# Diagonal blocks of the scores copied by ScalarE, and small sums moved behind a read of PSUM, in a two-layer graph kernel

## The chip, the cores and the metric

The kernel runs on one core of a Trainium2 chip. Time is device time in microseconds (us) of one execution; the profile is of one further execution and uses the hardware profiler's records. The engines are named as in the profile: PE is TensorE's matrix products, PEld its weight loads, DVE is VectorE, ACT is ScalarE, POOL is GpSimd, SP is SyncE, which here only issues transfers (DMAs). A trailing q (SPq, DVEq) means the engine's instruction queue and not its arithmetic.

## The reference

There are 64 graphs of 256 nodes with 512 features, one adjacency matrix of zeros and ones for all, and two residual layers with a layer norm and a ReLU ahead of each:

```python
h = jnp.maximum(_layernorm(x, axis=-1), 0.0)
q, k, v = h @ Wq.T, h @ Wk.T, h @ Wv.T
rel = adj.T[None] * einsum('bnd,bmd->bnm', q, k)
rel = rel / norm(rel, axis=2)
x = x + einsum('bnm,bmd->bnd', rel, v)          # layer 0
h = jnp.maximum(_layernorm(x, axis=-1), 0.0)
x = x + (einsum('nm,bmd->bnd', adj, h) @ weight + bias)   # layer 1
```

## The kernel before

The 64 graphs are worked through as 32 pairs. For a pair i the steps are: h, the norm of x; ht, its transpose; g, the product of h with the matrix m (which holds Wq and Wk multiplied beforehand); v, the product with Wv; the scores rel, from h and g; attention, which adds rel times v to x; h2, the second norm; y, the gather of h2 over the adjacency matrix; and the mix, which multiplies y with the weight and adds to x. Pairs overlap: `steady(i)` (L1009), called for i = 1 to 28, does attention and the second layer of pair i, the scores of pair i + 1, g and v of pair i + 2 and the transposes of pair i + 3. `first_pairs` and `last_pairs` (L1057) fill and drain this.

The large products are done by Winograd's scheme of seven products of half size with sums of blocks ahead of and behind them (`winograd_steps`, L187), and for g, v and mix two of the seven are split again (`two_levels`, L212). The seven are called a1, c5, a6, a7, a4 (large ones, into the PSUM banks bank_a and bank_c) and g1 to g4 (groups of small ones, into bank_d and bank_e). Each step issues its matmuls and then the instruction that reads the bank: ScalarE copies the first result for a block (`take`, L467 for g, L516 for v), VectorE adds a later one (L776 for mix). As bank_a is used again and again, a product into it waits until the bank has been read.

The order of every engine's instructions is written by hand and is kept as written (`manual_schedule`, L904). `run_steps` (L280) runs a list of steps, and behind step n it runs what the dictionary `side` has under n; "slot n" means that place. What waits for what is found by the framework from the pieces of tiles that instructions read and write, and becomes waits on semaphores.

The scores of a pair end in `rel`, 128 partitions (the row n within half k of the nodes) with all 256 columns m. Attention needs them transposed. VectorE's transpose (L592, `turn`) turns each 32x32 block on its own, so the blocks have to be moved first: block (j, k) of every 128x128 square goes from partitions 32k.. and columns 32j.. of `rel` to partitions 32j.. and columns 32k.. of `placed`. `place` (L584) does it with 16 transfers from SP's queue, one for each (j, k), each of 32 partitions x 8 runs of 32 numbers. In the 4 of them with j = k the partitions and columns don't change. Ahead of `place`, ScalarE has squared the scores into `placed` as a scratch (L570), taken the root, and scaled `rel` (L582). Behind it VectorE's four `turn`s write `turned`.

In `steady`, `place` is in slot 0 of `g_and_v` (L918), right behind the scaling; the turns are in slot 3 of the gather (`run_steps(y_products, ...)`, L1042), behind the last of y's four products. Just ahead of the turns on VectorE stands the first sum of y, L176 (slot 2); just behind it the second, L177, whose result mix's product c5 uses. `g_and_v` has seven steps: slot 5 lies behind v's c5 (ScalarE: v<-bank_c, L516) and slot 6 behind g's a4 and g3 (ScalarE: g<-bank_a, L467); next on ScalarE come the four copies of y out of PSUM (L746). SP's queue in an iteration holds 16 transfers of `place_blocks` (L443, from `h`), one load of x, and then the 16 of `place`; next it waits for the h of the next iteration.

In the tail, `second_of_y` (L758) gives eight small sums of y (128x128, L176 to L179), which the small products of mix take: the first four of the list hold the sums for g1, the last four those for g2 and g3. For the last two pairs (b and c in `last_pairs`) they are put into slots of the mix: four behind a1 and four behind c5 for pair b, all eight behind c5 for pair c.

Of the kernel before, what the change touches and what calls it, by code (L numbers as in the profile page):

```python
# [19 lines left out]
def kernel(  # L20
# [38 lines left out]
    nc = tc.nc  # L59
    P = 128  # L60
# [10 lines left out]
    S = 32  # L71
# [7 lines left out]
    small = ctx.enter_context(tc.tile_pool(name="small", bufs=3))  # L79
    ps_m = ctx.enter_context(tc.tile_pool(name="ps_m", bufs=8, space=bass.MemoryType.PSUM))  # L80

    X, H, HL, G, V, R, H2, Y, HL2, Y2, second_h = ({} for _ in range(11))

    ring = [const.tile([P, NB, NC, D], F32, name=f"x_ring{n}") for n in range(5)]
    blocks = const.tile([P, TC, DC, P], F32, name="blocks")
# [34 lines left out]
    def flat(t):  # L120
        return t.rearrange("p b c d -> p (b c) d")
# [154 lines left out]
    def winograd(product, take, side={}, early=False):  # L276

        run_steps(winograd_steps(product, take, early), side)
# [30 lines left out]
    def product_of_tokens(left, right):  # L309

        def product(bank, n, start):
            for b in range(NB):
                for d in range(HC):
                    nc.tensor.matmul(  # L314
                        bank[:, ts(b, P)], right[n][:, d, ts(b, P)], left[n][:, d, ts(b, P)],
                        start=(start and b == 0 and d == 0), stop=(d == HC - 1),
                        skip_group_check=True,
                    )
        return product
# [180 lines left out]
    def g_operands(i, room=None):  # L500

        g = G[i]
        if room is None:
            t = work.tile([P, 3, HC, HT_], F32, tag="ys", name=f"gt_{i}")
            room = [t[:, n] for n in range(3)]
        G[i], steps = right_operands(lambda j, k: g[:, j * HC : (j + 1) * HC, k], room)
        return steps
# [34 lines left out]
        products = v_products(i)  # L542
        return two_levels(*products, *second_weights_moving(HL2[i], wv_second, V[i]))

    def scores(i, side={}, by_matmul=False, inside=False):

        left, right = HL.pop(i), G.pop(i)
        rel = work.tile([P, NB, NC, N], F32, tag="rel", name=f"rel_{i}")  # L550
        placed = work.tile([P, NB, NC, NC, P], F32, tag="placed", name=f"placed_{i}")
        turned = work.tile([P, NB, NC, NC, P], F32, tag="turned", name=f"turned_{i}")
        rn = small.tile([P, NB, NC], F32, tag="rn", name="rn")
        R[i] = turned, rel, placed

        def take(t, k, bank, first):
            dst = rel[:, :, k, ts(t, P)]
            src = bank[:, :HT_].rearrange("p (b m) -> p b m", b=NB)
            if first:
                nc.scalar.copy(dst, src)  # L560
            else:
                nc.vector.tensor_add(dst, src, dst)  # L562

        def mask(k):
            nc.vector.tensor_mul(
                rel[:, :, k], rel[:, :, k], adjt_sb[:, k : k + 1, :].to_broadcast([P, NB, N])
            )

        def square_sum(b, k):
            nc.scalar.activation(  # L570
                placed[:, b, k].rearrange("p t n -> p (t n)"), rel[:, b, k], AF.Square,
                accum_out=rn[:, b, k : k + 1],
            )

        def root():
            nc.scalar.activation(rn, rn, AF.Sqrt)

        def inverse():
            nc.vector.reciprocal(rn, rn)

        def scale(b, k):
            nc.scalar.activation(rel[:, b, k], rel[:, b, k], AF.Copy, scale=rn[:, b, k : k + 1])  # L582

        def place():  # L584
            rv = rel.rearrange("p b k (t m) -> p (b k t) m", m=P)
            pv = placed.rearrange("p b k t n -> p (b k t) n")
            for j in range(P // S):
                for k in range(P // S):
                    nc.sync.dma_start(out=pv[ts(j, S), :, ts(k, S)], in_=rv[ts(k, S), :, ts(j, S)])  # L589

        def turn(b, k):
            nc.vector.transpose(turned[:, b, :, k], placed[:, b, k])  # L592

        def each(f):
            return [(lambda b=b, k=k: f(b, k)) for k in range(NC) for b in range(NB)]

        def turn_at_once():
            for b in range(NB):
                pt = ps_m.tile([P, T], F32, tag="pm", name="pr")
                for t in range(NC):  # L600
                    for k in range(NC):
                        nc.tensor.transpose(
                            pt[:, ts(t * NC + k, P)], rel[:, b, k, ts(t, P)], ident
                        )
                nc.scalar.copy(turned[:, b].rearrange("p t k n -> p (t k n)"), pt)

        masks, squares = [lambda: mask(0), lambda: mask(1)], each(square_sum)
        if inside:
            side = by_slot(side, {5: masks[1:], 6: squares[2:]})
            masks, squares = masks[:1], squares[:2]  # L610
        winograd(product_of_tokens(left, right), take, side)
        if by_matmul:
            return masks, squares, root, inverse, rn, turn_at_once
        return (
            masks, squares, root, inverse, each(scale), place,
            each(turn),
        )
# [185 lines left out]
    def by_slot(*works):  # L803

        side = {}
        for work_items in works:
            for n, items in work_items.items():
                side[n] = side.get(n, []) + list(items)
        return side
# [199 lines left out]
    def steady(i, exact, relu0, v_last, mixed, v):  # L1009

        gs = g_operands(i + 1)
        relus0 = relus_of_h(i + 3, relu0)
        stats, root, end, relus, uppers, lowers = ln1(i, exact)
        halves = [stats[b * NC + t] for t in range(NC) for b in range(NB)]
        attend_and_v(i, mixed, v, {
            0: relus0[0:2] + v_last, 1: relus0[2:4] + gs[0:1], 2: gs[1:2],
            3: gs[2:3], 4: gs[3:4] + halves[0:1], 5: halves[1:2],  # L1020
        })
        place_blocks(i + 3)
        if i + 4 < NP:
            load(i + 4)
        HL2.pop(i + 1)
        h_second = second_h.pop(i + 2)()
        masks, squares, norm_root, inverse, scales, place, turns = scores(i + 1, {
            0: halves[2:3], 1: halves[3:4] + h_second[0:1], 2: [root] + h_second[1:4],
            3: [end] + relus[0:1], 4: relus[1:2],
        }, inside=True)  # L1030
        turned, sums = transpose_blocks(i + 3)
        v_steps, rel_steps = attend_operands(i + 1)
        g, v = g_and_v(i + 2, {
            0: masks + squares + [norm_root] + turned[0:4] + [inverse] + scales + [place],
            1: uppers[0:2] + lowers[0:2],
            2: relus[2:4],
            3: uppers[2:4] + turned[4:8],
            4: lowers[2:3] + sums[0:1] + add_bias(i),
            5: lowers[3:4] + sums[1:3], 6: sums[3:4] + v_steps[0:1],
        })  # L1040
        y_products, y_steps = gather_steps(i, exact)
        run_steps(y_products, {0: v_steps[1:2], 2: y_steps[0:1], 3: turns})  # L1042
        y_second = second_of_y(i)
        totals, row_squares, mean, root0, end0, relu0 = [], [], [], [], [], None
        if i + 4 < NP:
            totals, *middle, relu0 = norm_by_scalar(flat(X[i + 4]))
            mean, row_squares, root0, end0 = [middle[0]], middle[1], [middle[2]], [middle[3]]
        run(y_steps[1:2])
        mixed = mix_and_v(i, g, v, {
            0: y_steps[2:4] + totals[0:2], 1: y_second[0:4] + totals[2:4],  # L1050
            2: y_second[4:8] + mean + row_squares[0:2],
            3: rel_steps[0:2] + row_squares[2:4], 4: root0 + rel_steps[2:4] + end0,
            5: v_steps[2:3],
        })
        return relu0, v_steps[3:4], mixed, v

    def last_pairs(exact, relu0, v_last, mixed, v):  # L1057

        a, b, c = NP - 3, NP - 2, NP - 1
        gs = g_operands(b)  # L1060
        stats, root, end, relus, uppers, lowers = ln1(a, exact)
# [18 lines left out]
        y_steps = gather(a, exact)  # L1080
# [6 lines left out]
        y_second = second_of_y(a, "hs2")  # L1087
# [7 lines left out]
        m = mix_by_two_levels(a)  # L1095
        root, end, relus, uppers, lowers = parts
# [9 lines left out]
        y_products, y_steps = gather_steps(b, exact)  # L1106
        run_steps(y_products, {2: y_steps[0:1]})
        y_second = second_of_y(b, "hs2")
# [5 lines left out]
        m = mix_by_two_levels(b)  # L1114
        root, end, relus, uppers, lowers = parts
# [1 line left out]
            m["a1"], m["c5"], m["a6"], m["g1"], lambda: run([m["a7"], m["c"]]), m["g2"], m["a4"],  # L1117
            m["g3"],
        ], {
            0: y_second[0:4] + [root], 1: y_second[4:8] + [end] + relus[0:2] + uppers[0:2],  # L1120
            4: lowers[0:2] + relus[2:4], 5: uppers[2:4] + add_bias(c), 7: lowers[2:4],
        })
        y_products, y_steps = gather_steps(c, exact)
        run_steps(y_products, {0: [m["g4"]], 2: y_steps[0:1]})
        y_second = second_of_y(c, "hs2")
        run(y_steps[1:2])
        m = mix_by_two_levels(c)
        run_steps([
            m["a1"], m["c5"], m["a6"], m["g1"], lambda: run([m["a7"], m["c"]]), m["g2"], m["a4"],
            m["g3"], m["g4"],  # L1130
        ], {0: y_steps[2:4], 1: y_second})

    first = dict(X), H[0]
    with tc.If(inexact < 1) as either:
# [33 lines left out]
```

## Time and profile before

| what | us |
|---|---|
| timed runs: median of 3 (lowest to highest) | 1706.56 (1706.11 to 1707.01) |
| the profiled execution: its own time | 1703.48 |
| its span, from first to last instruction | 1701.4 |
| PE busy in it | 1684.2 |
| DVE busy | 1472.9 |
| ACT busy | 811.3 |
| issue of one transfer placed<-rel on SP, least / median / most | 0.585 / 0.609 / 1.804 |
| from its issue to its landing, least / median / most | 1.9 / 2.0 / 4.0 |

A line in order of time has: start in us from the span's start, length in us, engine, source line, operation, output<-inputs by the program's names, shape, number of instructions put together, and in brackets the idle time of the engine ahead of it with what ended it. A line of the chain of waits has only start, length and what. In the busy table, x is the number of instructions. Matmuls are pipelined: the next one can start before the last has ended, so starts tell more than lengths. The granted TensorE clock was 0.999 of full speed.

### The profile page before, as it was taken

The numbers are of one execution on the slowest core, as the hardware profiler recorded it, in microseconds if no ns is written. First come the engines' busy times: TensorE is split into PE (matmuls) and PEld (weight loads), VectorE is DVE, ScalarE is ACT, GpSimd is POOL, SyncE is SP. The second block draws the span as 40 slices with busy tenths as digits, with TensorE's granted clock in tenths as the row PEclk, the third lists the DMA queues.
The fourth block names the chain that finished last, engine by engine and source line by source line (L and its number), as shares of the span: only waits on it lengthen the run. The fifth ranks groups of instructions, "written<-read, shape, count | busy, mean of one in ns | idle before, by whom it ended". The sixth has DMA issues, their size and how long they took to land.

```text
span 1701.4 us, 28459 instructions
## 1 busy us (share of the span) xinstructions
PE 1684.2 (99%) x10274; PEld 1530.6 (90%) x10274; DVE 1472.9 (87%) x3312; ACT 811.3 (48%) x1835; POOL 226.7 (13%) x191
## 2 busy tenths in 40 slices
PE   9999999999999999999999999999999999999997
PEld 7979999999899999999999999999999999999986
DVE  7788889888898888898888988888988889888677
ACT  4455444545445554445544455454455544453331
POOL 1211100111101111001111001110011110011111
PEclk9999999999999999999999999999999999999999
DMA  7414332234332233332343322443323433223101
GB/s 247 63 26 87 84 78 57 55 77 87 79 62 68 53 87 85 77 60 63 65 87 80 83 50 50 87 87 77 60 67 60 87 83 80 55 47 62 38 25 53
DMA packets 425734, 122.56 MB, mean 72 GB/s; under 512 B 398064, under 2 KB 398832, under 8 KB 425584
## 3 DMA queue, kind: packets, MB, share of 16 engines
q1 hardware_dynamic: 412992, 80.28, 25.6%
q0 software_dynamic: 8432, 32.51, 5.2%
q10 hardware_dynamic: 4160, 7.87, 1.3%
q8 instruction: 83, 1.36, 0.3%
q14 instruction: 67, 0.55, 0.1%
HBM read 38.27 MB, written 33.55 MB: 42 GB/s over the span
## 4 chain that ended last, share of the span: by engine, by line
PE 91%; DVE 4%; SPq 2%; DMA 1%; ACT 1%; issue 1%; DVEq 0%; ACTq 0%
PE bank_a L302 24%; PE bank_a L290 12%; PE bank_a L314 7%; PE bank_c L302 6%; PE bank_e L528 6%; PE bank_a L665 6%; PE py L742 6%; PE bank_d L528 5%; PE bank_c L314 3%; PE bank_c L290 3%; PE bank_c L665 3%; PE bank_e L481 3%; SPq L589 2%; PE bank_d L481 2%; PE bank_b L314 2%; PE bank_b L665 1%
## 5 line engine op out<-in xcount | busy, mean ns | idle before, releaser
L726 POOL TENSOR_TENSOR x_ring<-x_ring,bias_bc 128x512 f32<-128x512 f32 x128 | 187.2, 1483 | 667.3 <-DVE rel L562 406.2
L302 PE MATMUL bank_a<-wv_t,ht 128*128 128x256 f32 x768 | 181.7, 379 | 0.0
L290 PE MATMUL bank_a<-ht,m_t 128*128 128x256 f32 x768 | 181.4, 379 | 0.0
L290 PEld LDWEIGHTS bank_a<-ht,m_t 128*128 128x128 f32 x768 | 145.9, 190 | 19.8
L302 PEld LDWEIGHTS bank_a<-wv_t,ht 128*128 128x128 f32 x768 | 143.5, 190 | 18.3
L714 DVE TENSOR_TENSOR h<-h2c,h 128x512 fp32r<-128x512 f32 x128 | 85.4, 689 | 80.0 <-ACT h L710 80.0
L516 ACT COPY v<-bank_a 128x512 f32<-128x512 f32 x96 | 55.1, 574 | 206.5 <-PE bank_a L302 206.5
L367 ACT ACTIVATE blocks<-x_ring,sm 128x512 f32<-128x512 f32 x112 | 80.8, 722 | 125.3 <-DVE sm L364 123.5
L742 PE MATMUL py<-adjt_r,h 128*128 128x256 f32 x1024 | 127.1, 281 | 0.5 <-DVE h L714 0.4
L345 ACT ACTIVATE h2c<-x_ring,nb,rs 128x512 f32<-128x512 f32 x128 | 97.3, 809 | 58.0 <-DVE nb L342 51.9
L302 PE MATMUL bank_a<-w_t,ys 128*128 128x256 f32 x512 | 121.4, 380 | 2.2 <-DVE x_ring L776 2.2
L742 PEld LDWEIGHTS py<-adjt_r,h 128*128 128x128 f32 x1024 | 120.9, 189 | 1.0 <-DVE h L714 0.9
L797 POOL DMA_DIRECT2D out_dram<-x_ring x31 | 24.0, 773 | 723.3 <-issue 522.9
L380 ACT ACTIVATE h<-x_ring,nb,rs 128x512 f32<-128x512 f32 x112 | 82.0, 802 | 66.0 <-PE bank_e L528 66.0
L302 PEld LDWEIGHTS bank_a<-w_t,ys 128*128 128x128 f32 x512 | 96.7, 190 | 16.4 <-DVE x_ring L776 3.0
L746 ACT COPY yt<-py 128x512 f32<-128x512 f32 x128 | 74.9, 588 | 70.4 <-PE py L742 47.3
L776 DVE TENSOR_TENSOR x_ring<-bank_a,x_ring 128x512 f32<-128x512 f32 x128 | 87.9, 687 | 23.2 <-PE bank_a L302 23.2
L314 PE MATMUL bank_a<-ht,gt 128*128 128x128 f32 x744 | 101.2, 279 | 0.0
L333 DVE BATCH_NORM_STATS2 st<-x_ring 128x6 f32<-128x512 f32 x144 | 97.6, 678 | 0.4
L560 ACT COPY rel<-bank_a 128x256 f32<-128x256 f32 x96 | 35.7, 372 | 129.6 <-PE bank_a L314 111.1
L314 PEld LDWEIGHTS bank_a<-ht,gt 128*128 128x128 f32 x744 | 90.4, 192 | 2.8
L453 DVE STREAM_TRANSPOSE ht<-blocks 128x256 f32<-128x256 f32 x248 | 87.7, 407 | 0.7 <-DMA blocks<-h 0.7
(223 smaller groups left out, 4012.5 us busy)
## 6 DMA issues: line engine op xcount, KB each, us to landing
blocks<-h SPq DMA_DIRECT2D x496, 64.0 KB, 2.3
out_dram<-x_ring POOLq DMA_DIRECT2D x31, 1024.0 KB, 4.8
x_ring<-in_x_dram SPq DMA_DIRECT2D x28, 1024.0 KB, 5.6
placed<-rel SPq DMA_DIRECT2D x496, 32.0 KB, 2.0
x_ring<-in_x_dram ACTq DMA_DIRECT2D x4, 1024.0 KB, 5.3
wq_sb<-in_L_gnn_Wq_dram SPq DMA_DIRECT2D x4, 256.0 KB, 4.8
wk_sb<-in_L_gnn_Wk_dram ACTq DMA_DIRECT2D x4, 256.0 KB, 6.0
wv_sb<-in_L_gnn_Wv_dram ACTq DMA_DIRECT2D x1, 1024.0 KB, 5.6
```

Of the source, the lines that this page charges most:

```text
L290: nc.tensor.matmul(bank[:, e * HT_ : (e + 1) * HT_], right[n][:, d, ts(e, P)], left[n][:, d, :], start=(start and e == 0 and d == 0), stop ...
L302: nc.tensor.matmul(bank[:, b * HD : (b + 1) * HD], left[n][:, d, ts(b, P)], right[n][:, d, :], start=(start and b == 0 and d == 0), stop=( ...
L314: nc.tensor.matmul(bank[:, ts(b, P)], right[n][:, d, ts(b, P)], left[n][:, d, ts(b, P)], start=(start and b == 0 and d == 0), stop=(d == H ...
L333: nc.vector.bn_stats(st[:, c, :], src[:, c, :])
L345: nc.scalar.activation(dst, src[:, c, :], AF.Relu, bias=nb[:, c : c + 1], scale=rs[:, c : c + 1])
L453: nc.vector.transpose(ht[:, d, half].rearrange("p (b n) -> p b n", b=NB), by_half[:, :, half, d])
L528: nc.tensor.matmul(out, left[k][n], right[k][n], start=start, stop=True, skip_group_check=True)
L665: nc.tensor.matmul(bank[:, ts(b, HD)], left[n][:, b], right[n][:, b], start=(start and b == 0), stop=True, skip_group_check=True,)
L714: nc.vector.tensor_sub(dst[:, 1, c, :], whole_h[c], dst[:, 0, c, :].bitcast(F32))
L726: (lambda c=c: add(xt[:, c, :], xt[:, c, :], bias_bc, ALU.add)) for c in range(TC)
L742: nc.tensor.matmul(pm[:, d, :], left[:, b * NC + m, ts(d0 + d, P)], right, start=(n == 0), stop=(n == len(terms) - 1),)
L776: nc.vector.tensor_add(xt[block], bank.rearrange("p (b e) -> p b e", b=NB), xt[block])
```

## The change

Two edits. In `steady`, the scores are called with `own=True`: `place` then leaves out the four transfers with j = k, and four ScalarE copies of the same blocks (`stay`) are put into slots 5 and 6 of `g_and_v`, two in each, ahead of the other side work there. `first_pairs` and `last_pairs` keep the 16 transfers. In `last_pairs`, the eight small sums of y move back by one slot: for pair b from slots 0 and 1 to slots 1 and 2, for pair c the last four from slot 1 to slot 2. What is computed doesn't change.

```diff
-    def scores(i, side={}, by_matmul=False, inside=False):
+    def scores(i, side={}, by_matmul=False, inside=False, own=False):
...
+        rv = rel.rearrange("p b k (t m) -> p (b k t) m", m=P)
+        pv = placed.rearrange("p b k t n -> p (b k t) n")
+
         def place():
-            rv = rel.rearrange("p b k (t m) -> p (b k t) m", m=P)
-            pv = placed.rearrange("p b k t n -> p (b k t) n")
             for j in range(P // S):
                 for k in range(P // S):
-                    nc.sync.dma_start(out=pv[ts(j, S), :, ts(k, S)], in_=rv[ts(k, S), :, ts(j, S)])
+                    if j != k or not own:
+                        nc.sync.dma_start(
+                            out=pv[ts(j, S), :, ts(k, S)], in_=rv[ts(k, S), :, ts(j, S)]
+                        )
+
+        def stay(j):
+            nc.scalar.copy(pv[ts(j, S), :, ts(j, S)], rv[ts(j, S), :, ts(j, S)])
+
+        own_steps[i] = [(lambda j=j: stay(j)) for j in range(P // S)]
...
-        }, inside=True)
+        }, inside=True, own=True)
...
-            5: lowers[3:4] + sums[1:3], 6: sums[3:4] + v_steps[0:1],
+            5: own_steps[i + 1][0:2] + lowers[3:4] + sums[1:3],
+            6: own_steps[i + 1][2:4] + sums[3:4] + v_steps[0:1],
...
-            0: y_second[0:4] + [root], 1: y_second[4:8] + [end] + relus[0:2] + uppers[0:2],
+            0: [root], 1: y_second[0:4] + [end] + relus[0:2] + uppers[0:2], 2: y_second[4:8],
...
-        ], {0: y_steps[2:4], 1: y_second})
+        ], {0: y_steps[2:4], 1: y_second[0:4], 2: y_second[4:8]})
```

More of the change, by code (lines that the diff above doesn't have):

```diff
@@ L80 @@
     ps_m = ctx.enter_context(tc.tile_pool(name="ps_m", bufs=8, space=bass.MemoryType.PSUM))
-    X, H, HL, G, V, R, H2, Y, HL2, Y2, second_h = ({} for _ in range(11))
+    X, H, HL, G, V, R, H2, Y, HL2, Y2, second_h, own_steps = ({} for _ in range(12))
     ring = [const.tile([P, NB, NC, D], F32, name=f"x_ring{n}") for n in range(5)]
```

## The prediction

> **What bounds the kernel now.** I read the page first, then the chain of waits, then one iteration of the steady loop and the tail in order of time. From the page, busy time and the chain that ended last:
>
> ```profile
> PE 1684.2 (99%) x10274; PEld 1530.6 (90%) x10274; DVE 1472.9 (87%) x3312; ACT 811.3 (48%) x1835; POOL 226.7 (13%) x191
> ...
> PE 91%; DVE 4%; SPq 2%; DMA 1%; ACT 1%; issue 1%; DVEq 0%; ACTq 0%
> ```
>
> TensorE sets the end, and a change of the copies and transfers is worth only the moments at which TensorE waits. SP's queue and the transfers hold 3% of the chain, but that is an alternative route through the same time: it counts only where its end is late. So I looked at the end of that route, at 628 to 634 us (the chain in order of time: start, length, what):
>
> ```profile
> 628.42 1.32 SPq L589
> ...
> 629.79 1.93 DMA placed<-rel
> ...
> 631.90 0.16 DVE turned L592
> ...
> 632.26 1.05 DVE turned L592 x3
> 633.32 0.58 DVE yt L177
> 633.90 0.14 issue
> 634.04 0.46 PE bank_c L302
> ```
>
> The sixteenth transfer is issued at 629.79, lands 1.93 later, and only then VectorE does the four transpositions, the sum L177 and with it TensorE's product c5. How often is VectorE really idle before the first of them? The answer for L592 from 200 to 1570 us, what its engine sat idle for (us, times):
>
> ```profile
>   DMA placed<-rel: 1.4, 3
>   issue: 0.9, 2
> ```
>
> Five of the 28 steady iterations, 2.3 us in all. In the other 23 the last transfer landed before VectorE was through with L176, and the transposition started 0.08 before L176's recorded end; so a late one costs its idle time and 0.08 more. As a check, the first transpositions of successive iterations stand 51.72 us apart when undisturbed, and 52.19, 52.37, 52.15, 52.37 and 52.34 ahead of those five (at 268.6, 424.6, 631.9, 1149.8 and 1512.5): 0.47 + 0.65 + 0.43 + 0.65 + 0.62 = 2.8 us. The delay is not made good later.
>
> In the tail, the last mix, in order of time:
>
> ```profile
> 1685.75 0.68 DVE L776 TENSOR_TENSOR x_ring<-bank_c,x_ring 128x512 f32<-128x512 f32 x1
> 1686.35 0.28 DVE L176 TENSOR_TENSOR ys<-yt 128x128 f32<-128x128 f32 x1
> ...
> 1688.26 0.29 DVE L179 TENSOR_TENSOR ys<-ys,ys 128x128 f32<-128x128 f32 x1
> 1688.46 0.68 DVE L776 TENSOR_TENSOR x_ring<-bank_a,x_ring 128x512 f32<-128x512 f32 x1
> ...
> 1689.20 1.99 PE L302 MATMUL bank_a<-w_t,ys 128*128 128x256 f32 x8 [1.14 <-DVE x_ring L776]
> ```
>
> Eight small sums, 1686.35 to 1688.46, stand between two reads of PSUM, and product a7 waits for the second read. The mix before it does the same at 1670.74 (0.78 shown there as idle).
>
> **What the skill says.** "ScalarE: Activation LUTs", What ACT_TABLE_LOAD costs: an ACTIVATE with immediate scale takes 186 ns + 0.833 ns per element, and neighbours overlap by about 93 ns. That gives 399 ns for 256 elements, or 306 ns from start to start. The trace agrees: the 128x256 copies of L560 take 372 and the squares of L570 412. "DMA: Bandwidth & Descriptors", Anatomy of one DMA: about 2.0 us of a transfer do not depend on its size; the table of issues has a median of 2.0 for placed<-rel. "VectorE: DVE Perf Modes", The three transpose paths: the engine transposes 32x32 blocks on its own, and the rest must be moved. The diagonal blocks therefore need no change of partition, and a ScalarE copy can stand in for their transfer.
>
> **The change, part by part.**
>
> 1. Transfers out. 28 iterations lose four of 16 issues; one takes a median of 0.609 us and follows the last by about 0.65. SP's list ends 4 x 0.65 = 2.6 us earlier. Undisturbed, the first transfer of an iteration is issued 12.57 us before the transposition and the last issue ends 2.2 before it; now it ends 4.8 before. With the slowest landing of the trace, 4.0 us from issue, less 0.6 of issue, it is there 1.4 us before VectorE asks. The five late turns were late by at most 0.65, so 2.6 earlier covers all: gain 2.8 us. SP's freed time is worth nothing: behind these transfers it waits for ScalarE's relus of the next iteration (L443, 555.6 us of waiting over 28 times).
>
> 2. Copies in. 4 x 28 = 112 ScalarE copies of 32 partitions x 256 elements, two behind v's c5 copy and two behind g's a4 copy. The cover is in ScalarE's own timeline:
>
> ```profile
> 625.72 0.58 ACT L516 COPY v<-bank_c 128x512 f32<-128x512 f32 x1 [1.93 <-PE bank_c L302]
> 627.44 0.58 ACT L467 COPY g<-bank_a 128x512 f32<-128x512 f32 x1 [1.14 <-PE bank_a L290]
> 629.26 0.59 ACT L746 COPY yt<-py 128x512 f32<-128x512 f32 x1 [1.23 <-PE py L742]
> ```
>
> The two holes are 1.14 and 1.23 us and each ends with TensorE. A pair costs 0.31 + 0.40 = 0.71. It fits with 0.43 and 0.52 to spare: cost nothing. The trace has no copy with 32-element runs between SBUF tiles. From below it can't be cheaper than about 0.27, the shortest start to start of an L560 copy; from above I allow twice the price, a pair of 1.5. Then g's copy starts at 627.8, the second pair follows, the first yt copy at 629.8 and the second at 630.3, ready at 630.9. L176 started at 630.87, so even this costs only about 0.1 us x 28 = 3 us. I take nothing.
>
> 3. The added wait. The first transposition now also waits for ScalarE's fourth copy; behind it on VectorE are L177 and the read of bank_a, and TensorE's c5 waits for L177. The copy ends near 628.03 + 0.71 = 628.7, L176 at 631.55, so 2.8 us to spare. What is late next, in every iteration: VectorE's own backlog. TensorE keeps some 0.18 us ahead of c5 (101 + 75 ns beyond the pitch of its matmuls at 581.9 and 582.2), which is not touched.
>
> 4. Tail, last mix. The read of a6's bank now comes after four small sums: VectorE is there at 1687.41. A6 was started at 1685.28; a7, which started at 1689.20 and was read at 1691.23, shows 2.03 us from a product's start to its read, so a6 is ready at 1687.31. The read starts at 1687.41 instead of 1688.46, and a7, 0.74 later, at 1688.15 instead of 1689.20: 1.05 us. The other four sums (1.06 us) now push the reads of bank_e and bank_d to 1689.1 and 1689.4. The next products need them free at 1689.9 and 1690.3: 0.3 us to spare, nothing lost. The factors of the first four sums, wanted by g1's last matmul at 1687.67, are there at 1687.49.
>
> 5. Tail, mix before it. All eight sums move behind one read each. VectorE then goes: c5's read at about 1667.1, four sums 1667.7 to 1668.7, reciprocal and nb to 1669.0, a6's read when a6 is ready, 1667.08 + 2.03 = 1669.11 (was 1670.01), a7 at 1669.84 (was 1670.74): 0.9 us. TensorE's g1 ends at 1669.80, so no more is to be had. nb is done about 1 us earlier too, so ScalarE's relus behind it follow along, and the shift reaches the end.
>
> Sum: 2.8 + 0 + 1.05 + 0.9 = 4.75 us. The profiled execution took 1703.48 (span 1701.4), so it would take 1698.7. The median of the timed runs, 1706.56, is 3.1 above that execution; I keep the offset and get **1701.8 us**. Should those 3.1 us be six more late turns, they would go too, down to 1698.7.
>
> **Rivals.**
>
> *More late turns in the timed runs.* They are not profiled, and a landing late by half a microsecond is chance. For: the 3.1 us have no other visible cause. Against: the timed runs lie within 0.9 us of each other. Time 1698.7 to 1700.7.
>
> *Only the tail pays.* Something else holds the transposition in the iterations where the transfers were late, or the copies at twice their price eat the gain (part 2: 2.8 against 3). For: two of the five late starts are put down to "issue", not to a landing. Gain 1.95, time 1704.6.
>
> *The copies wait for the transfers; slower.* If the program orders the copies behind the landing of the twelve transfers into the same tile, the first pair starts not at 626.3 but at 618.9 + 12 x 0.65 + 1.3 = 628.0, and g's a4 copy and all yt copies behind it slip: L176 by 0.2 us, bank_a by 1.3, of which TensorE feels perhaps half. At 0.5 us an iteration that is 14 us: 1706.6 - 4.75 + 14 = 1716. It decides from 4.75 / 28 = 0.17 us an iteration on. Against: the sixteen transfers, interleaved pieces of the same tile, go out 0.65 apart although each takes 2.0 to land, so pieces that don't touch are not ordered among themselves.
>
> *Nothing comes of it.* The tail's reads wait for another thing and new late turns take the place of the old: 1706.5.
>
> **How the numbers follow.** Both gains at the offset of today 0.57 (own range 1700.8 to 1702.9); more late turns 0.16; only the tail 0.12; slower 0.10; nothing 0.05. A measurement of this kernel can't tell less than 0.2%, 3.4 us, from no change. Below 1703.15: 0.57 + 0.16 = 0.73. Within: 0.12 + 0.05 = 0.17. Above 1709.97: 0.10. From 1699.0 to 1705.0 the range leaves out the slower case, the nothing case and the lowest part of the second, under 2 in 10.
>
> **What would show it.** After: 384 transfers placed<-rel instead of 496, 112 new ScalarE copies of about 0.4 us; L592 idle for no transfer in the steady iterations, which then stand an even 51.7 apart; ScalarE's holes before g's and yt's copies smaller by 0.7 but still ended by TensorE; the idle of a7 at the two tail places down from 0.78 and 1.14 to about 0.1. I am wrong if a new copy shows a wait for a transfer, if g's a4 copy follows the second new copy without a hole, or if L592's idle stays with another releaser.

## The result, and the profile after

| | before | changed |
|---|---|---|
| timed runs, median (lowest to highest), 9 each | 1705.83 (1705.18 to 1707.01) | 1701.02 (1700.33 to 1702.44) |
| the profiled execution: its own time | 1703.48 | 1700.89 |
| its span | 1701.4 | 1699.1 |

The ratio is 0.9973, with a 95% interval of 0.9963 to 0.9983. The medians lie 4.81 us apart, by the interval between 2.9 and 6.3, where 4.75 was predicted; the predicted time was 1701.8. The two profiled executions lie only 2.6 us apart, though, and that is the first sign that the sum came out right for reasons that were not all the predicted ones.

Busy time and the chain that ended last, on the page of the changed kernel:

```profile
PE 1685.2 (99%) x10274; PEld 1530.6 (90%) x10274; DVE 1474.9 (87%) x3312; ACT 856.7 (50%) x1947; POOL 227.1 (13%) x191
...
PE 96%; DVE 3%; DMA 0%; issue 0%; ACT 0%; ACTq 0%; DVEq 0%
```

The route over SP's queue and the transfers (3% before) is gone, and ScalarE has 112 instructions and 45 us more. The answer for the four transpositions, now L602, from 200 to 1570 us:

```profile
L602 DVE STREAM_TRANSPOSE turned<-placed x108: 398/404/447, 217.3 to 1563.5; 128x256 f32<-128x256 f32 x108
its engine sat idle before it (us, times) until:
who waited for it (us, times):
```

Nothing stands under the second line: VectorE is not idle ahead of any transposition in the loop. They now follow each other at 51.73 to 51.77 us in every iteration. ScalarE's list at the same place of the loop as was shown of before, in order of time:

```profile
625.50 0.59 ACT L516 COPY v<-bank_c 128x512 f32<-128x512 f32 x1 [1.92 <-PE bank_c L302]
625.98 0.83 ACT L597 COPY placed<-rel 32x256 f32<-32x256 f32 x2
627.23 0.59 ACT L467 COPY g<-bank_a 128x512 f32<-128x512 f32 x1 [0.42 <-PE bank_a L290]
627.84 0.83 ACT L597 COPY placed<-rel 32x256 f32<-32x256 f32 x2
629.04 0.59 ACT L756 COPY yt<-py 128x512 f32<-128x512 f32 x1 [0.37 <-PE py L752]
```

The copies sit in the two holes; 0.42 and 0.37 us are left, and TensorE still ends both. They wait for no transfer.

The last mix of the tail did what was predicted: between c5's read and a7's start there were 3.45 us before (1685.75 to 1689.20) and are 2.40 now:

```profile
1684.49 0.68 DVE L786 TENSOR_TENSOR x_ring<-bank_c,x_ring 128x512 f32<-128x512 f32 x1
...
1686.89 1.99 PE L302 MATMUL bank_a<-w_t,ys 128*128 128x256 f32 x8
```

Pair b's mix did not. Before, in order of time:

```profile
1669.19 0.28 DVE L178 TENSOR_TENSOR ys<-ys 128x128 f32<-128x128 f32 x1
...
1672.57 0.61 PE L528 MATMUL bank_e<-w_t,ys 128*128 128x128 f32 x4
```

And in the changed kernel:

```profile
1667.91 1.99 PE L302 MATMUL bank_a<-w_t,ys 128*128 128x256 f32 x8
...
1668.11 2.68 POOL L736 TENSOR_TENSOR x_ring<-x_ring,bias_bc 128x512 f32<-128x512 f32 x2 [14.68 <-DVE ys L178]
1668.30 1.37 DVE L178 TENSOR_TENSOR ys<-ys 128x128 f32<-128x128 f32 x1
...
1669.71 1.24 DVE L179 TENSOR_TENSOR ys<-ys,ys 128x128 f32<-128x128 f32 x1
...
1671.33 0.71 PE L528 MATMUL bank_e<-w_t,ys 128*128 128x128 f32 x4 [1.42 <-DVE x_ring L537]
```

Product a7 starts without a wait, as predicted. But two of the small sums, 0.28 us each before, take 1.37 and 1.24 while GpSimd adds the bias to pair c, and the next product, g2, waits 1.42. To compare executions I measure from a6's start in this mix to the start of g3, where the bank_e reads have caught up: 1667.08 to 1675.65 before, 8.57 us; 1665.14 to 1674.39 now, 9.25. The edit to pair b has cost 0.68 us. For the whole tail I take the time from the first transposition of the last steady iteration to the end of the span: 137.1 us before (1564.3 to 1701.4), 136.6 now.

### The profile page after: what moved, and what is told of

Its sections match the earlier page's. It is cut to its first block, busy times and chain, and to the rows that moved or that the text cites. A ratio compares the mean times of both kernels' runs of the same rounds, so it can differ in the third digit from the quotient of the medians.

```text
span 1699.1 us, 28457 instructions
## 1 busy us (share of the span) xinstructions
PE 1685.2 (99%) x10274; PEld 1530.6 (90%) x10274; DVE 1474.9 (87%) x3312; ACT 856.7 (50%) x1947; POOL 227.1 (13%) x191
## 3 DMA queue, kind: packets, MB, share of 16 engines
q8 instruction: 83, 1.36, 0.3%
## 4 chain that ended last, share of the span: by engine, by line
PE 96%; DVE 3%; DMA 0%; issue 0%; ACT 0%; ACTq 0%; DVEq 0%
PE bank_a L302 25%; PE bank_a L290 13%; PE bank_a L314 7%; PE py L752 7%; PE bank_c L302 7%; PE bank_e L528 6%; PE bank_a L675 6%; PE bank_d L528 5%; PE bank_c L290 3%; PE bank_c L314 3%; PE bank_e L481 3%; PE bank_c L675 3%; PE bank_d L481 2%; PE bank_b L314 2%; PE bank_b L675 1%; PE pu L636 1%
## 5 line engine op out<-in xcount | busy, mean ns | idle before, releaser
L724 DVE TENSOR_TENSOR h<-h2c,h 128x512 fp32r<-128x512 f32 x128 | 85.5, 691 | 80.1 <-ACT h L720 80.1
```

The lines of the kernel that those rows point to most:

```text
L724: nc.vector.tensor_sub(dst[:, 1, c, :], whole_h[c], dst[:, 0, c, :].bitcast(F32))
```

## The experiments

Two theories stood after this. **A**: the loop gained more in the timed runs than the profiled execution shows, as their transpositions were late more often, and pair b's edit loses because GpSimd's addition holds up the sums. **B**: the predicted sum, 2.8 from the loop and 1.95 from the tail, with the small difference of the two profiled executions being chance. All times below are medians of timed runs; each group was run beside the kernel before, whose median was 1705.32, 1706.92 and 1706.15 in the three groups. Differences from it are therefore made within a group, and where two kernels of different groups are compared, their profiles decide.

**The loop alone.** The tail's two slot lists go back to those of before:

```diff
-            0: [root], 1: y_second[0:4] + [end] + relus[0:2] + uppers[0:2], 2: y_second[4:8],
+            0: y_second[0:4] + [root], 1: y_second[4:8] + [end] + relus[0:2] + uppers[0:2],
...
-        ], {0: y_steps[2:4], 1: y_second[0:4], 2: y_second[4:8]})
+        ], {0: y_steps[2:4], 1: y_second})
```

> The transfers and copies of the steady loop alone, the tail as before. Theory A (the profile of the change: late transfers cost 2.7 us in the profiled execution and more in the timed runs, and the tail edit nets only 0.35 us): 4.4 us below the kernel before, near 1701.4. Theory B (the sum on record: 2.8 from the loop, 1.95 from the tail): 2.8 us below, near 1703.0. Both: no idle time of L602 for a transfer in the steady iterations, which stand 51.73 us apart.

Measured: 1700.85, 4.5 us below (ratio 0.9975, 0.9965 to 0.9984), span 1698.5, no idle time ahead of any transposition from 200 to 1570 us. The point is A's, though the interval (2.7 to 6.0 us) just reaches B's 2.8. The tail takes 137.1 us, as before.

**The tail alone.** `own=True` and the copies are taken out:

```diff
-        }, inside=True, own=True)
+        }, inside=True)
...
-            5: own_steps[i + 1][0:2] + lowers[3:4] + sums[1:3],
-            6: own_steps[i + 1][2:4] + sums[3:4] + v_steps[0:1],
+            5: lowers[3:4] + sums[1:3],
+            6: sums[3:4] + v_steps[0:1],
```

> The moved small sums alone, with 16 transfers and no copies in the loop. Theory A: 1.05 us gained in the last mix, 0.7 lost in the mix before it, net 0.35 us, within what can be measured; in the profile two of the small sums of pair b take over 1 us each. Theory B: 1.95 us below the kernel before. The loop keeps its late transpositions, some 5 of 28 in the profile.

Measured: 1704.76, 0.6 us below, ratio 0.9998 (0.9990 to 1.0007): no difference that can be told, and B's 1.95 lies outside the interval (1.2 above to 1.7 below). The tail takes 136.8 us, 0.4 less than before, and two sums of pair b take 1.37 and 1.24 us here too. This run has the 16 transfers of before, and its profiled execution is a second look at how often they are late. What VectorE was idle for ahead of L602, from 200 to 1570 us (us, times):

```profile
  DMA placed<-rel: 3.0, 6
  issue: 1.0, 2
```

Eight times and 4.0 us, where the execution shown ahead of the prediction had five and 2.3. From the first to the last transposition of steady it is 1401.7 us here, 1399.55 in that execution and 1396.89 in the changed kernel: the same 16 transfers cost 4.8 us in one execution and 2.7 in the other. So the number of late transpositions differs between executions, and the one profiled before was a lucky one: its own time, 1703.48, lies below every timed run of that kernel (the lowest is 1703.91), while this one's, 1705.84, lies in their midst. The timed runs' larger gain fits that; their transpositions can't be seen.

**Pair b's sums back, all else as changed.**

```diff
-            0: [root], 1: y_second[0:4] + [end] + relus[0:2] + uppers[0:2], 2: y_second[4:8],
+            0: y_second[0:4] + [root], 1: y_second[4:8] + [end] + relus[0:2] + uppers[0:2],
```

> The changed kernel with the small sums of pair b back in slots 0 and 1; the loop and pair c as changed. Theory A: 0.7 us below the changed kernel (6.19 us from a6's start to g2's in pair b's mix go back to 5.49). Theory B: 0.9 us above the changed kernel.

Measured: 1699.74, 5.6 us below the kernel before; a6 to g3 takes 8.57 again, and the tail 136.0 us against 136.6 with the change. B's 0.9 us above the change is not what happened. From the loop alone it differs by pair c's edit only: the tail is 1.1 us shorter than there (136.0 and 137.1), which is the predicted 1.05. The timed medians differ by 1.1 too, but that is within their scatter.

**Pair c's second norm finished later.** The bias addition waits for the first relu and the relu for `nb`; both come one read later:

```diff
-            0: [root], 1: y_second[0:4] + [end] + relus[0:2] + uppers[0:2], 2: y_second[4:8],
+            0: [root], 1: y_second[0:4], 2: [end] + relus[0:2] + uppers[0:2] + y_second[4:8],
```

> The changed kernel with the reciprocal and nb of pair c's second norm, and the relus behind them, moved from ahead of a6's read to behind it, so that GpSimd's bias addition, which follows the first relu, starts about 0.9 us later. Theory A (GpSimd's addition holds up the small sums, which read two operands from SBUF): the sums of pair b take 0.28 us each again, g2 follows a7 without a wait, 1.6 us below the changed kernel, near 1699.4. Rival (the sums are long for another reason): the sums stay over 1 us and the time stays within 0.3 us of the changed kernel.

Measured: 1699.03, 6.3 us below the kernel before (ratio 0.9964, 0.9951 to 0.9978), and in the profiles the tail is 1.1 us shorter than with the change (135.5 and 136.6). In order of time:

```profile
1667.90 0.28 DVE L178 TENSOR_TENSOR ys<-ys 128x128 f32<-128x128 f32 x1
...
1669.06 0.61 PE L528 MATMUL bank_e<-w_t,ys 128*128 128x128 f32 x4
...
1672.52 0.71 PE L528 MATMUL bank_e<-w_t,ys 128*128 128x128 f32 x4 [0.52 <-DVE x_ring L537]
```

The sum is short again and g2 (1669.06) follows a7 (1667.23) by 1.83. Part of it comes back one product later: g3 waits 0.52 and starts 3.46 behind g2, not 3.08 as before, because two subtractions of the second norm (L724, until 1672.13) now stand ahead of the read of bank_e on VectorE. A6 to g3: 8.07.

**No bias addition while the sums run.** First I took the wrong one, `add_bias(b)`, which GpSimd makes one mix earlier; the expectation speaks of pair c, but the edit was to pair b's:

```diff
-            4: lowers[0:2] + relus[2:4], 5: uppers[2:4] + add_bias(b), 7: lowers[2:4],
+            4: lowers[0:2] + relus[2:4], 5: uppers[2:4], 7: lowers[2:4],
```

> The changed kernel without the four bias additions of pair c on GpSimd (the result of that pair is left without its bias; nothing else is left out). Theory A (GpSimd's addition holds up the small sums of pair b): the two long sums take 0.28 us each, g2 follows a7 1.83 us after it as in the kernel before pair b's edit would allow, and the span is 1.5 us shorter than the changed kernel's. Rival (the sums are long for another reason): no difference over 0.3 us.

Measured: 1700.16 (6.8 us below the kernel before, which took 1706.92 in this group), span 1698.4. The sums of pair b still take 1.36 and 1.24 us beside an addition of 2.69, and g2 waits 1.42. It decides nothing. The right one:

```diff
-            4: lowers[0:2] + relus[2:4], 5: uppers[2:4] + add_bias(c), 7: lowers[2:4],
+            4: lowers[0:2] + relus[2:4], 5: uppers[2:4], 7: lowers[2:4],
```

> The changed kernel without the four bias additions of pair c, those that GpSimd makes while pair b's mix runs (the result of pair c is left without its bias, nothing else is left out). The run without pair b's additions had taken out the wrong ones. Theory A (GpSimd's addition holds up the small sums): the two long sums take 0.28 us each, g2 starts 1.83 us after a7 without a wait, and from a6's start in pair b's mix to g3's it is 9.25 less 1.6, about 7.7 us. Rival (the sums are long for another reason): they stay over 1.2 us.

Measured: 1698.01, 8.1 us below the kernel before (ratio 0.9951, 0.9936 to 0.9966), span 1696.2. In order of time:

```profile
1667.52 0.28 DVE L178 TENSOR_TENSOR ys<-ys 128x128 f32<-128x128 f32 x1
1667.84 0.29 DVE L179 TENSOR_TENSOR ys<-ys,ys 128x128 f32<-128x128 f32 x1
...
1668.96 0.61 PE L528 MATMUL bank_e<-w_t,ys 128*128 128x128 f32 x4
```

With no work on GpSimd and the same instructions on VectorE, both sums are short and g2 follows a7 (1667.13) by 1.83, at once. A6 to g3 takes 7.68 us, which is 8.57 less 0.89: the gain that the prediction had put down for pair b is there as soon as GpSimd is out of the way.

**The loop's copies taken away**, both they and the four transfers missing:

```diff
-            5: own_steps[i + 1][0:2] + lowers[3:4] + sums[1:3],
-            6: own_steps[i + 1][2:4] + sums[3:4] + v_steps[0:1],
+            5: lowers[3:4] + sums[1:3],
+            6: sums[3:4] + v_steps[0:1],
```

> The changed kernel without the 112 ScalarE copies; the diagonal blocks of placed then hold the squares that were put there as a scratch, so the scores of 28 pairs are not computed rightly, all else is. If the copies lie wholly in ScalarE's holes: the same as the changed kernel within 0.3 us, near 1700.5 to 1701, iterations 51.73 us apart. If they cost something: faster, by up to 28 x 0.1 = 3 us.

Measured: 1700.60, 6.3 us below the kernel before (3.9 to 7.7), where with the copies it was 4.8 (2.9 to 6.3) in another group, so the timed runs can't settle it. The profiles do: span 1699.1 with and without; from the first to the last transposition of steady 1396.89 us with and 1396.67 without. By these, the copies cost 0.2 us at most.

**The copies twice.**

```diff
-            5: own_steps[i + 1][0:2] + lowers[3:4] + sums[1:3],
-            6: own_steps[i + 1][2:4] + sums[3:4] + v_steps[0:1],
+            5: own_steps[i + 1][0:2] * 2 + lowers[3:4] + sums[1:3],
+            6: own_steps[i + 1][2:4] * 2 + sums[3:4] + v_steps[0:1],
```

> The changed kernel with each pair of copies issued twice, four in slot 5 and four in slot 6. A group then takes 4 x 0.42 = 1.7 us in holes of 1.14 and 1.23. By the reckoning on record (L176 late once a group takes more than 1.45): L176 starts 2 x 1.7 - 2.9 = 0.5 us late in every iteration, 28 x 0.5 = 14 us, near 1715. If ScalarE has more slack than its holes: under 3 us more than the changed kernel.

Measured: 1714.81, 14.2 above the run without copies in the same group (against the kernel before: 1.0051, 1.0036 to 1.0067). In order of time:

```profile
631.16 0.59 ACT L467 COPY g<-bank_a 128x512 f32<-128x512 f32 x1
...
631.77 1.68 ACT L597 COPY placed<-rel 32x256 f32<-32x256 f32 x4
...
634.58 0.69 DVE L176 TENSOR_TENSOR ys<-yt 128x512 f32<-128x512 f32 x1 [0.38 <-ACT yt L756]
```

ScalarE now runs from one copy into the next without a hole, y's copies stand behind it, and VectorE is idle ahead of L176 until one of them ends. Iterations are 52.20 apart instead of 51.73: 28 x 0.47 = 13 us. So the cover is real and has an end, and the prediction's reckoning finds it.

**Four transfers more.** In the kernel before, the transfers of j = 0 once more behind the 16:

```diff
-    def scores(i, side={}, by_matmul=False, inside=False):
+    def scores(i, side={}, by_matmul=False, inside=False, again=False):
...
                     nc.sync.dma_start(out=pv[ts(j, S), :, ts(k, S)], in_=rv[ts(k, S), :, ts(j, S)])
+            for k in range(P // S if again else 0):
+                nc.sync.dma_start(out=pv[ts(0, S), :, ts(k, S)], in_=rv[ts(k, S), :, ts(0, S)])
...
-        }, inside=True)
+        }, inside=True, again=True)
```

> The kernel before, with the four transfers of j = 0 issued once more behind the 16 in each of the 28 steady iterations, 20 in all. If the end of SP's list gates the transpositions: it ends 2.6 us later, 0.4 us behind the present start of the first transposition, the last landing comes 1.3 us after, so every transposition is 1.7 to 1.8 us late and the iterations stand 53.5 us apart: 28 x 1.75 = 49 us above the kernel before less the 5 it loses already, near 1750. If there is other slack: within 10 us of the kernel before.

Measured: 1794.87 over two runs (1.0518, 1.0472 to 1.0565), 89 us above. What VectorE was idle for ahead of the transpositions, from 200 to 1650 us (us, times):

```profile
  DMA placed<-rel: 66.1, 26
```

The first transposition waits in every iteration, 2.54 us on average and not 1.75. The 20 issues take 13.6 us and not 13.0, and 1.6 and not 1.3 pass from the last issue to the transposition. That makes 28 x 2.54 = 71 us. The profiled execution took 1803.30, 100 us more than the one before, with a granted TensorE clock of 0.983. The clock is where the rest is: in 14 of the 28 iterations it stood at 0.50 for 3.4 or 6.8 us around the late c5; elsewhere in the loop it was at full speed. C5's eight matmuls in one iteration with such a stretch and in one without, in order of time:

```profile
672.61 3.75 PE L302 MATMUL bank_c<-w_sb,yt 128*128 128x256 f32 x8 [2.92 <-DVE yt L177]
...
729.18 1.97 PE L302 MATMUL bank_c<-w_sb,yt 128*128 128x256 f32 x8 [1.85 <-DVE yt L177]
```

These stretches are 58 us together; half of it, 29 us, is lost, and 71 + 29 = 100. In the traces with 16 and 12 transfers none is found in the loop. What length of wait brings one on can't be read off: waits with one are 1.9 to 3.3 us long, waits without one 1.7 to 3.0 us. The theory holds in kind: 16 transfers just fit, 20 do not, 12 leave room.

**One step on: v's sum later.** In the kernel with the later second norm, a sum of v's blocks leaves VectorE's backlog ahead of c5:

```diff
-        run_steps(y_products, {0: v_steps[1:2], 2: y_steps[0:1], 3: turns})
+        run_steps(y_products, {2: y_steps[0:1], 3: turns})
...
-            3: rel_steps[0:2] + row_squares[2:4], 4: root0 + rel_steps[2:4] + end0,
+            3: v_steps[1:2] + rel_steps[0:2] + row_squares[2:4], 4: root0 + rel_steps[2:4] + end0,
```

> The kernel with the later reciprocal and nb for pair c, and in the loop one sum of v's blocks (L135, 0.69 us of VectorE) moved from ahead of y's first sum into slot 3 of the mix. If VectorE's backlog is what is late next at c5 (0.18 us in every iteration): L177 starts about 0.15 us sooner, and the iterations stand 51.57 us apart, 28 x 0.15 = 4 us less, near 1695. If something else sets c5, or the sum delays a later product by as much: within 1 us of 1699.0, or above it.

Measured: 1697.35, 9.6 us below the kernel before (ratio 0.9946, 0.9933 to 0.9960), the fastest of all; by the spans 1.5 us below the kernel that it starts from (1697.2 to 1695.7). Iterations stand 51.67 us apart on average instead of 51.73, so about a third of the 0.15 came. In order of time:

```profile
629.66 0.69 DVE L176 TENSOR_TENSOR ys<-yt 128x512 f32<-128x512 f32 x1 [0.61 <-ACT yt L756]
...
632.45 1.92 PE L302 MATMUL bank_c<-w_sb,yt 128*128 128x256 f32 x8
```

VectorE now waits for y and not y for VectorE, and c5 follows its neighbour (630.73) by 1.72, without a wait. So it already did in some iterations of the kernel that this one starts from, in those whose gather took 4.01 us:

```profile
265.10 4.01 PE L752 MATMUL py<-adjt_r,h 128*128 128x256 f32 x32
268.95 1.89 PE L302 MATMUL bank_a<-w_sb,yt 128*128 128x256 f32 x8
270.68 1.94 PE L302 MATMUL bank_c<-w_sb,yt 128*128 128x256 f32 x8
```

There the gather takes 4.01 us in 10 of the 28 iterations and 3.88 to 3.90 in the others, here in 8 of 28; why isn't known, but it isn't the edit. After a short gather c5 was 0.10 late (1.83 behind its neighbour), after a long one not at all. Over all iterations the distance fell from 1.79 to 1.74 us, and that 0.05 is the gain. The other part of the 0.18, from c5's start to a6's, stayed at 1.79: it was not VectorE's backlog. So the promise was too large; nothing took it back.

**The bias additions in another order**, to keep the early norm and still start GpSimd late:

```diff
-            0: [root], 1: y_second[0:4], 2: [end] + relus[0:2] + uppers[0:2] + y_second[4:8],
-            4: lowers[0:2] + relus[2:4], 5: uppers[2:4] + add_bias(c), 7: lowers[2:4],
+            0: [root], 1: y_second[0:4] + [end] + relus[0:2] + uppers[0:2], 2: y_second[4:8],
+            4: lowers[0:2] + relus[2:4], 5: uppers[2:4] + [add_bias(c)[n] for n in (1, 0, 2, 3)], 7: lowers[2:4],
```

> The kernel with v's sum moved, with the reciprocal and nb of pair c's second norm back ahead of a6's read as in the change, and the four bias additions of pair c in the order 1, 0, 2, 3, so that the first one waits for the second relu. Theory A: GpSimd starts 0.7 us later than in the changed kernel, the small sums take 0.28 us (the last may start beside it), and g3's wait for the late sums of the second norm, 0.52 us with the later reciprocal, goes back: 0.4 us below the run with v's sum moved. If the order is not kept or the last sum is caught: one sum over 1 us and up to 1 us above it.

Measured: 1698.92, span 1697.1, so 1.4 us of span above the run with v's sum moved, 1.1 of it in the tail. GpSimd starts 0.90 us after the first relu does, as in the change (1668.11 after 1667.21), and the sums take 1.36 and 1.24. The order of GpSimd's work isn't written by hand in this kernel; whether it was put back or the waits were the same in either order isn't known. So a loss of this size again goes with the early addition, but the idea itself remains untried.

## Why the prediction was right, point by point

**Transfers out (2.8 us).** Right in mechanism: no transposition waits any more, and in the profiled executions the loop from the first to the last transposition of steady is 2.66 us shorter (1399.55 to 1396.89). Undersized for the timed runs: the loop alone gave 4.5 (2.7 to 6.0), and the difference from the kernel before, less what each kernel's tail gained in its profile, is 4.3 to 6.0 us in all seven kernels with 12 transfers in the loop and v's sum in its place (the one with the copies twice left out). The step that failed is the sum itself, five late ones counted in one execution. The rival "more late turns in the timed runs" was the truer account of this half. What was held against it, that the timed runs lie within 0.9 us, rested on three runs: the 45 later ones of the same kernel reach from 1703.91 to 1708.90. Nor is a late landing the usual cause: in four of the five late iterations one issue on SP took 1.1 to 1.8 us instead of 0.61, so that the 16 took 11.2 to 11.6 and not 10.4; only at 424.6 was the list on time and the landing late.

**Copies in (nothing).** Right; the price was a little off. One copy takes 0.402 us, close to the 0.399 estimated from the Trainium skill ("ScalarE: Activation LUTs", What ACT_TABLE_LOAD costs), but a pair takes 0.83 and not 0.71: these two start 0.41 to 0.43 apart, without the overlap of 0.09 that the sum took from that section. Taking the copies out changed 0.2 us at most, and doubling them cost 14.2 us where the same reckoning gave 14.

**The added wait (nothing).** Right. The fourth copy ends 2.6 us ahead of the transposition.

**Last mix (1.05).** Right to the hundredth in the profile (3.45 to 2.40), and 1.1 by the tails of two kernels that differ in nothing else.

**Pair b's mix (0.9).** Wrong: 0.68 lost. The step that failed is the sentence that `nb` comes 1 us earlier and the relus follow along. So they do, and the bias addition on GpSimd follows them, to 2.97 us after a6's start instead of 4.03 (1668.11 less 1665.14; 1671.11 less 1667.08 before). The small sums, put later, are then still under way. The part left VectorE's durations as they were and never asked who else starts earlier. The Trainium skill, "SBUF — State Buffer", Who interferes with whom, says that a VectorE instruction with two inputs in SBUF contends with a GpSimd instruction that reads SBUF, and that one with at most one such input, outside the two-port modes, doesn't. The runs agree: 0.28 became 1.37 beside the addition and was 0.28 without it, and the second long sum ends (1670.95) 0.16 behind GpSimd (1670.79). A read of PSUM with one input in SBUF took 0.41 beside the addition in the kernel before (L537 at 1671.13), as it does without it. The trace of before had shown the contention, in order of time in the loop:

```profile
612.84 0.68 DVE L565 TENSOR_TENSOR rel<-rel,adjt_sb 128x512 f32<-128x512 f32 x1
612.92 3.42 POOL L726 TENSOR_TENSOR x_ring<-x_ring,bias_bc 128x512 f32<-128x512 f32 x2 [15.08 <-DVE rel L562]
...
613.97 1.23 DVE L565 TENSOR_TENSOR rel<-rel,adjt_sb 128x512 f32<-128x512 f32 x1 [0.45 <-ACT rel L560]
```

The first L565, which starts 0.08 ahead of GpSimd, takes 0.68; the second, started beside it, 1.23.

**The sum.** 4.75 was predicted and 4.81 came, out of about 4.5 from the loop (1.7 more than predicted) and 0.4 from the tail by the profiles (1.6 less). That is luck: two errors of one size and opposite sign made the number look better than its parts. The kept offset of 3.1 us was most likely late transpositions, at least in part: with the 2.1 us by which the loop of the tail-alone run was longer, the profiled execution before would have taken 1705.6, where its timed runs lie. Most of the offset is gone: the changed kernel's median is 0.1 above its profiled execution, and before's 2.4.

**The smaller gain between the two profiled executions** is thus explained by the lucky one of before, with a further 0.9 us ahead of the loop: the first transposition of steady came at 165.61 after 164.72. It varied from 164.82 to 165.69 among the kernels with 12 transfers in the loop; the cause is open.

## What to carry to other kernels

When a wait depends on when transfers are issued and land, one profiled execution gives one draw of it: compare the profiled execution's own time with the timed runs, and if it is the fastest, expect the wait to be larger than it shows. When an edit makes a result ready earlier, follow it to every engine that was waiting for it, GpSimd above all, and look which of VectorE's instructions with two SBUF inputs will then lie beside its work. A longer duration of the same instruction and shape elsewhere in the trace is the place to see the price beforehand.

## What was not expected of the hardware

Two neighbouring copies of 32 partitions from SBUF to SBUF start 0.41 to 0.43 us apart, more than their length of 0.402, while behind a 128x256 copy out of PSUM, 0.37 long, the next instruction starts 0.27 after it (L560 at 613.57, L570 at 613.84 before). Four more transfers of 32 KB in each iteration brought, beside the waits for them, 14 stretches of half the TensorE clock in the profiled execution, where the kernel before had none in its loop; the second timed run of that kernel, 1786.43, shows a mean clock of 0.990 against 0.983. And the gather's 32 matmuls take 3.88 to 3.90 us in some iterations and 4.01 in others, in 11 of 28 before and in 2 of 28 in the changed kernel, with no wait shown; after a long one c5 starts without its wait, so that the iteration stays as long as it was (51.74 us after a short one and 51.73 after a long one in the changed kernel).
